# Layer 3's weighted sums of eight heads as 128x64 column tiles in one TensorE run over two PSUM banks

## The chip, the cores and the metric

The kernel runs on one core of a Trainium2 chip. The metric is device time in microseconds (us) of that core for one launch. The median of three runs of the kernel before is 3227.3 us (3219.42 to 3229.8). A core has four engines that compute (TensorE, called PE in the profile; VectorE, DVE; ScalarE, ACT; GpSimd, POOL) and SyncE (SP), which here only issues DMAs. Each runs its own queue of instructions in order. A matrix product on TensorE is two kinds of instruction: a weight load (LDWEIGHTS, shown as PEld) of the operand called `lhsT`, and a MATMUL that streams the other operand, `rhs`, past it into a bank of PSUM. All data here is fp32, for which one matrix product of the program becomes two weight loads and two MATMULs, so the counts in the profile are twice those in the code.

## The reference, cut to what matters

Four graph attention layers run one after another on 128 independent graphs of 128 nodes with 512 features, each as `x = x + layer(relu(layernorm(x)))`. The change is in layer 3, which has eight heads (H = 8) of 64 features (k = 64):

```
xp = jnp.einsum('bnd,do->bno', x, W_proj)
xh = xp.reshape(B, N, H, k).transpose(0, 2, 1, 3)
a_src = jnp.einsum('bhnk,hk->bhn', xh, W_att[:, :k])
a_dst = jnp.einsum('bhnk,hk->bhn', xh, W_att[:, k:])
scores = a_src[:, :, :, None] + a_dst[:, :, None, :] + b_att[None, :, None, None]
scores = jax.nn.leaky_relu(scores, negative_slope=NEG_SLOPE)
mask = (A > 0)[:, None, :, :]
scores = jnp.where(mask, scores, NEG_INF)
att = jax.nn.softmax(scores, axis=-1)
out = jax.nn.relu(jnp.einsum('bhij,bhjk->bhik', att, xh))
return out.transpose(0, 2, 1, 3).reshape(B, N, H * k)
```

The changed step is the last einsum: for each graph and each head, a 128x128 matrix of attention weights times a 128x64 matrix of features.

## The kernel before, in words

A graph is handled whole: its 128 nodes lie on the 128 partitions, and one graph passes through all four layers in a coroutine (`graph`, line 1053), which yields one step at a time. Up to 13 graphs (`FLYING`) are in flight together. The order in which the instructions of all of them are put into the queues is made when the program is built, by a list scheduler (`Scheduler`, line 158): it keeps an estimate of when each engine is free and when each buffer is written, and takes among the steps that could start next on an engine the one of best rank, where a step's rank comes from its graph's number and its due time in a rehearsed plan. The estimates come from `Step.estimate` (line 70); for a PE product it returns `2 * max(0.00084 * columns, 0.108)` us (line 85). A `Group` (line 106) is a list of steps that is issued in one go, with nothing of another graph between them. A buffer is asked for with `Take` and freed with `give_back`; the eight PSUM banks are one such pool (`bank()`, line 387).

`layer3` (line 909) does, for one graph: the normalisation; four transposes of `h`; the projection (`projected`, tiles `bank<-wpx,ht` in the profile) into `fx`, which holds per head two score columns, 64 features and a column of ones; the scores of all heads in one tile `e` of 128x1024; mask, leaky ReLU and exponential on DVE and ACT; and a transposition of `e` by DMA and DVE (by TensorE for the last five graphs, `late`). Then `et[k]` is the transposed 128x128 matrix of head k.

The weighted sums follow (lines 985 to 1009). They go in two halves of four heads. For each half one bank is taken, and one `Group` of four products is issued: `lhsT` is `et[k]` (128x128, as weights), `rhs` is `fx[:, k, E3:]` (65 columns: the features and the ones, whose sum is the softmax's denominator), the result 128 partitions by 65 columns. In the profile these are `bank<-x,e` with 128x65, or `bank<-x,ht` for the last five graphs. When a half is in its bank, DVE takes the reciprocal of the four denominators (line 1002) and multiplies (line 1003) into `t`, and the bank is given back before the coroutine asks for the second. Each graph has two such halves, so the kernel has 256 groups of four products, 1024 products, 2048 weight loads and 2048 MATMULs of this kind. The scheduler may put other graphs' work between the two halves, and mostly does.

Other names that stand below: `bank<-w1x,ht` is layer 1's projection, `bank<-et,xl` its weighted sums, `bank<-w2x,y` its second projection, `bank<-h,et` and `bank<-x,et` the weighted sums of the layers with one head, `bank<-ident,h` transposes. All instructions of the coroutines carry line 310 in the profile (312 in the changed file), since the scheduler issues them there, so they are told apart by their tiles.

Of the kernel before, what the change touches and what calls it, by code (L numbers as in the profile page):

```python
# [42 lines left out]
def size(ap):  # L43
    n = 1
    for count in ap.shape[1:]:
        n *= count
    return n


class Step:  # L50
# [19 lines left out]
    def estimate(self, name, outs, ins, kw):  # L70

        if name == "dma_start":
            moved = size(outs[0]) * outs[0].shape[0] * 4
            if self.engine == "POOL":
                self.moves = moved / 165e3
                return 1.0, 3
            run = 4 * min(a.shape[-1] for a in outs + ins)
            self.moves = moved / (280e3 if run > 512 else 220e3 if run > 128 else 130e3)
            busy = 0.5 if max(len(a.shape) for a in outs + ins) > 2 else 0.35
            return busy, (2.2 if moved > 16384 else 1.3)  # L80
        n = max(size(a) for a in outs[:1] + ins)
        if self.engine == "PE":
            if name == "transpose":
                return 0.109, 0.2
            return 2 * max(0.00084 * size(outs[0]), 0.108), 0.2
        if self.engine == "DVE":
            if name == "bn_stats":
                return 0.6, 0.12
            if name == "bn_aggr":
                return 0.09, 0.12  # L90
            per = 1 / 960
            if name == "tensor_scalar" and n >= 256:
                per /= 2
            return n * per + 0.07, 0.12
        if self.engine == "ACT":
            pointers = sum(isinstance(kw.get(k), bass.AP) for k in ("bias", "scale"))
            busy = n * 0.00081 + 0.105 + (0, 0.075, 0.135)[pointers]
            return busy + 0.1 * ("accum_out" in kw), 0.15
        if self.engine == "POOL":
            if kw.get("op") == ALU.pow or ALU.pow in kw.get("ops", ()):  # L100
                return 0.6, 0.1
            return (0.25 if n <= 16 else 0.55 if name == "tensor_scalar" else 1.3), 0.1
        raise ValueError(name)
# [54 lines left out]
class Scheduler:  # L158
# [14 lines left out]
    def give_back(self, *aps):  # L173
        for ap in aps:
            name = ap.tensor.name
            tag = self.tag_of.pop(name)
            heapq.heappush(self.returned[tag], self.last_use.get(name, 0.0))
# [157 lines left out]
def kernel(  # L335
# [24 lines left out]
    B, P, D = x.shape  # L360
# [4 lines left out]
    H3 = l3_watt.shape[0]  # L365
    K3 = l3_watt.shape[1] // 2
# [12 lines left out]
    T = Engine("PE", nc.tensor)  # L379
# [5 lines left out]
    give_back = sched.give_back  # L385

    def bank():
        return Take(ps, [P, 512], "bank", 8)

    def tile_of(tag, bufs, *shape):  # L390
        return Take(work, [P, *shape], tag, bufs)
# [15 lines left out]
    E1, E2, E3 = 2 * H1, 2, 2  # L407
# [151 lines left out]
    def norm_relu(xt):  # L559

        n = nc.vector.BN_STATS_DIM
        st = yield tile_of("st", 6, n + 5)
        yield V.bn_stats(st[:, :n], xt)
        mean, var = st[:, n : n + 1], st[:, n + 1 : n + 2]
        yield V.bn_aggr(st[:, n : n + 2], st[:, :n])
        ve, rstd, nmr = (st[:, i : i + 1] for i in range(n + 2, n + 5))
        yield G.tensor_scalar(ve, var, EPS, None, ALU.add)
        yield G.tensor_tensor(out=rstd, in0=ve, in1=minus_half, op=ALU.pow)
        yield G.tensor_scalar(nmr, mean, rstd, -1.0, ALU.mult, ALU.mult)
        h = yield tile_of("h", 4, D)  # L570
        yield A.activation(out=h, in_=xt, func=AF.Relu, bias=nmr, scale=rstd)
        give_back(st)
        return h
# [14 lines left out]
    def blocks_of(t):  # L588

        return [t[:, i : i + P] for i in range(0, t.shape[1], P)]  # L590
# [318 lines left out]
    def layer3(xt, mask, late):  # L909

        h = yield from norm_relu(xt)
        ht = yield from transposed(blocks_of(h), "ht", 3)
        give_back(h)
        yield Until("wp")

        fx = yield tile_of("x3", 3, H3, E3 + K3 + 1)
        yield G.memset(fx[:, :, E3 + K3 :], 1.0)
        half = H3 // 2
        yield from projected(
            ht,  # L920
            KC,
            [w.rearrange("p h k -> p (h k)") for w in wpx],
            2,
            [fx[:, g : g + half, : E3 + K3] for g in (0, half)],
        )
        give_back(ht[0])
        f = yield tile_of("f3", 4, 4, H3)
        f, mx, rz = f[:, :2], f[:, 2], f[:, 3]
        yield G.tensor_tensor(f, fx[:, :, :E3].rearrange("p h s -> p s h"), b_l3, ALU.add)

        e = yield tile_of("e3", 3, H3 * P)
        if late:
            heads = e.rearrange("p (h c b) -> p h c b", h=H3, b=Q)
        else:
            heads = e.rearrange("p (c h b) -> p h c b", h=H3, b=Q)
            rows = yield from rows_in_dram(repeated(f[:, 0]), H3)
            yield S.dma_start(out=e.rearrange("p (c f) -> p c f", c=R), in_=rows)
        mask3 = mask.rearrange("p (c b) -> p c b", b=Q)

        for g in range(0, H3, 4):  # L940
            part = [heads[:, g + j] for j in range(4)]
            if late:
                pt = yield from spread(f[:, 0, g : g + 4])
                part = pt.rearrange("p (h c b) -> p h c b", h=4, b=Q)
                part = [part[:, j] for j in range(4)]
            yield Group(
                [
                    V.tensor_tensor_reduce(
                        out=heads[:, g + j],
                        in0=part[j],  # L950
                        in1=mask3,
                        scale=1.0,
                        scalar=LOWEST,
                        op0=ALU.add,
                        op1=ALU.max,
                        accum_out=mx[:, g + j : g + j + 1],
                    )
                    for j in range(4)
                ]
            )  # L960
            if late:
                give_back(pt)
        give_back(mask)
        yield G.tensor_tensor(mx, mx, f[:, 1], ALU.add)
        yield A.activation(out=mx, in_=mx, func=AF.Prelu, alpha=SLOPE)
        yield G.tensor_scalar(mx, mx, -1.0, None, ALU.mult)
        for bias, func in ((f[:, 1], dict(func=AF.Prelu, alpha=SLOPE)), (mx, dict(func=AF.Exp))):
            for k in range(H3):
                yield A.activation(
                    out=heads[:, k], in_=heads[:, k], bias=bias[:, k : k + 1], **func  # L970
                )
        et = []
        if late:
            for g in range(0, H3, 4):
                et += yield from transposed(blocks_of(e)[g : g + 4], "ht", 3)
        else:
            to = yield from exchanged(e, "et3", 2)

            yield V.transpose(
                e.rearrange("p (h r b) -> p r h b", h=H3, b=Q),  # L980
                to.rearrange("p (r h b) -> p r h b", h=H3, b=Q),
            )
            give_back(to)
            et = blocks_of(e)
        t = yield tile_of("t", 5, D)
        for i in range(2):
            pa = yield bank()
            p3 = pa[:, : half * (K3 + 1)].rearrange("p (h k) -> p h k", h=half)
            yield Group(
                [  # L990
                    T.matmul(
                        p3[:, k - i * half, :],
                        lhsT=et[k],
                        rhs=fx[:, k, E3:],
                        start=True,
                        stop=True,
                    )
                    for k in range(i * half, (i + 1) * half)
                ]
            )  # L1000
            r = rz[:, i * half : (i + 1) * half]
            yield V.reciprocal(r, p3[:, :, K3])
            yield V.tensor_tensor(
                t[:, i * half * K3 : (i + 1) * half * K3].rearrange("p (h k) -> p h k", k=K3),
                p3[:, :, :K3],
                r.unsqueeze(2).to_broadcast([P, half, K3]),
                ALU.mult,
            )
            give_back(pa)
        give_back(e, fx, f)  # L1010
        if late:
            give_back(et[0], et[4])
        yield V.scalar_tensor_tensor(xt, t, 0.0, xt, ALU.max, ALU.add)
        give_back(t)
# [133 lines left out]
```

## Time and profile before

| what | value | where from |
|---|---|---|
| median of three runs | 3227.3 us (3219.42 to 3229.8) | the times |
| time of the profiled execution | 3227.98 us | the times |
| its span, first to last instruction | 3226.2 us | the page |
| mean granted TensorE clock | 0.994 | view of the cores |
| weight loads, busy | 2497.0 us (77%), 15386 instructions | the page |
| ACT busy | 2468.5 us (77%), 7224 | the page |
| POOL busy | 855.9 us (27%), 2313 | the page |
| chain that ended last | PE 91%, DVE 3%, DMA 3%, ACT 1%, issue 1% | the page |
| DVE, reciprocal of four denominators (`f<-bank`) | 256 of 173 ns | groups by form |
| DVE, multiplication of a half (`t<-bank,f`) | 256 of 411 ns | groups by form |

How to read it: the page gives for each engine the time in which it executed something. For PE that is not the same as running at its peak: MATMULs are pipelined, one starts before the one before it has ended, so the time that a MATMUL costs is the distance from its start to the next start (called its pitch below), not its duration. The pitch is read from the timeline, which lists runs of equal instructions with their starts.

### The profile page before, as it was taken

To read this page: it belongs to the slowest core of one execution; us is meant where nothing else is said; L and a number is where in the kernel's file an instruction comes from. 1 tells how busy PE (TensorE), PEld (TensorE's weight loads), DVE (VectorE), ACT (ScalarE), POOL (GpSimd) and SP (SyncE) were. 2 spreads that over 40 slices of the span, in tenths; PEclk is the share of its full clock that TensorE was granted. 3 is DMA by queue.
4 is the path that set the end of the run, shared out by engine and by line. 5 is a ranking of instruction groups with operands and counts; after the bars stand their busy time and mean duration, and the time that the engine had idled before them with its cause. 6 is when DMAs were issued, how large, how long until landed. Compare 5 with 4: busy or idle time off the path is not lost.

```text
span 3226.2 us, 60294 instructions
## 1 busy us (share of the span) xinstructions
PE 3189.4 (99%) x15386; PEld 2497.0 (77%) x15386; DVE 2857.0 (89%) x11663; ACT 2468.5 (77%) x7224; POOL 855.9 (27%) x2313
## 2 busy tenths in 40 slices
PE   8999999999999999999999999999999999999998
PEld 6777777777777777777777777777777777777786
DVE  6888888999998989999998999998999989989876
ACT  5677777778777877777877777777777777778867
POOL 1232222222222222222222222222222222222222
PEclk8999999999999999999999999999999999999999
DMA  6245555556556656655555555555555655555432
GB/s 173 52 114 137 144 143 152 153 150 154 150 144 157 153 141 155 155 144 155 155 146 141 157 153 151 153 152 141 151 151 151 154 150 149 143 159 149 110 101 66
DMA packets 770082, 460.39 MB, mean 143 GB/s; under 512 B 344776, under 2 KB 702408, under 8 KB 769736
## 3 DMA queue, kind: packets, MB, share of 16 engines
q1 hardware_dynamic: 765560, 456.53, 54.6%
q8 instruction: 123, 2.02, 0.3%
q14 instruction: 223, 1.83, 0.2%
q10 hardware_dynamic: 4176, 0.02, 0.1%
HBM read 299.00 MB, written 157.33 MB: 141 GB/s over the span
## 4 chain that ended last, share of the span: by engine, by line
PE 91%; DVE 3%; DMA 3%; ACT 1%; issue 1%; POOL 0%; SPq 0%; ACTq 0%; DVEq 0%; POOLq 0%
PE bank L310 91%; DVE e L310 1%; DMA e<-d 1%; DMA d<-r 1%; DMA row<-d 1%; DMA et<-exchanged 0%; DVE st L310 0%; POOL st L310 0%; SPq L310 0%; DVE products L310 0%; DVE xt L310 0%; ACT e L310 0%; DVE t L310 0%; DVE y L310 0%; ACT ht L310 0%
## 5 line engine op out<-in xcount | busy, mean ns | idle before, releaser
L310 PE MATMUL bank<-w2x,y 128*128 128x257 f32 x4096 | 968.6, 381 | 1.7 <-DVE y L310 1.7
L310 PE MATMUL bank<-w1x,ht 128*128 128x344 f32 x3072 | 953.9, 454 | 2.6 <-ACT ht L310 2.6
L310 PEld LDWEIGHTS bank<-w2x,y 128*128 128x128 f32 x4096 | 763.9, 190 | 157.3 <-issue 32.8
L310 PEld LDWEIGHTS bank<-w1x,ht 128*128 128x128 f32 x3072 | 570.3, 191 | 257.2 <-issue 9.3
L310 ACT ACTIVATE e<-e,f 128x128 f32<-128x128 f32 x2176 | 707.2, 390 | 3.1 <-DVE c L310 3.1
L310 POOL TENSOR_SCALAR st<-st 128x1 f32<-128x1 f32 x1024 | 311.1, 308 | 1185.8 <-DVE st L310 993.9
L310 ACT ACTIVATE e<-e,c 128x128 f32<-128x128 f32 x1408 | 533.1, 394 | 116.9 <-DVE c L310 60.2
L310 PE MATMUL bank<-wpx,ht 128*128 128x264 f32 x2048 | 497.1, 386 | 0.3 <-ACT ht L310 0.3
L310 ACT ACTIVATE h<-xt,st 128x512 f32<-128x512 f32 x512 | 411.3, 810 | 83.9 <-POOL st L310 74.4
L310 PEld LDWEIGHTS bank<-wpx,ht 128*128 128x128 f32 x2048 | 387.8, 190 | 97.9 <-issue 22.2
L310 DVE CUSTOM_DVE_ANT_0 e<-e,m 128x128 f32<-128x128 f32 x1484 | 337.8, 286 | 23.5 <-DMA e<-d 23.3
L310 DVE BATCH_NORM_STATS2 st<-xt 128x6 f32<-128x512 f32 x512 | 340.8, 679 | 0.5 <-DMA xt<-in_x_dram 0.5
L310 POOL TENSOR_TENSOR st<-st,minus_half 128x1 f32<-128x1 f32 x512 | 297.0, 599 | 23.6 <-POOL st L310 0.2
L310 PEld LDWEIGHTS bank<-x,e 128*128 128x128 f32 x1968 | 254.8, 191 | 62.2 <-issue 29.8
L310 PEld LDWEIGHTS bank<-et,xl 128*128 128x128 f32 x2048 | 264.7, 192 | 36.5 <-issue 8.8
L310 PE MATMUL bank<-et,xl 128*128 128x128 f32 x2048 | 270.1, 275 | 0.4 <-ACT et L310 0.4
L310 PE MATMUL bank<-h,et 128*128 128x512 f32 x512 | 263.8, 598 | 3.3 <-ACT et L310 1.9
L310 PE MATMUL bank<-x,e 128*128 128x65 f32 x1968 | 246.8, 268 | 8.5 <-DVE e L310 2.1
L310 ACT COPY xl<-bank 128x344 f32<-128x344 f32 x384 | 167.7, 437 | 108.1 <-PE bank L310 103.9
L310 ACT COPY ht<-bank 128x512 f32<-128x512 f32 x274 | 159.6, 582 | 114.9 <-PE bank L310 113.7
L310 ACT ACTIVATE t<-t 128x512 f32<-128x512 f32 x256 | 160.3, 627 | 88.1 <-DVE t L310 87.3
L310 DVE TENSOR_TENSOR y<-bank,b 128x512 f32<-128x512 f32 x256 | 175.1, 684 | 36.0 <-PE bank L310 34.7
(85 smaller groups left out, 4342.4 us busy)
## 6 DMA issues: line engine op xcount, KB each, us to landing
e<-d SPq DMA_DIRECT2D x123, 512.0 KB
exchanged<-e SPq DMA_DIRECT2D x492, 128.0 KB
et<-exchanged SPq DMA_DIRECT2D x123, 512.0 KB
xt<-in_x_dram SPq DMA_DIRECT2D x128, 256.0 KB
out_dram<-xt SPq DMA_DIRECT2D x128, 256.0 KB
e<-d SPq DMA_DIRECT2D x125, 256.0 KB
exchanged<-e SPq DMA_DIRECT2D x480, 64.0 KB
et<-exchanged SPq DMA_DIRECT2D x120, 256.0 KB
```

The costliest lines, as they stand in the source:

```text
L310: method(*args, **kw)
```

## The change

The two groups of four products become one group of sixteen. Both banks are taken before the group. Each head's product is split by its weights: columns 0 to 63 of `et[k]` give output partitions 0 to 63, columns 64 to 127 give output partitions 64 to 127 of the same bank and columns. So a product has 128x64 weights and a 64x65 result, and its place among the array's columns is given by the output's partitions. The 65 columns of `rhs` are streamed for each half. The order is head by head, low half and high half alternating, first the four heads of one bank, then those of the other. The two reciprocals and the two multiplications on DVE are the same as before; they now both come after the whole group. The planner's estimate gets a price of its own for a product with fewer than 128 output partitions, 0.07 us.

```diff
@@ -82,6 +82,8 @@
         if self.engine == "PE":
             if name == "transpose":
                 return 0.109, 0.2
+            if outs[0].shape[0] < 128:
+                return 0.07, 0.2
             return 2 * max(0.00084 * size(outs[0]), 0.108), 0.2
@@ -983,21 +985,22 @@
         t = yield tile_of("t", 5, D)
-        for i in range(2):
-            pa = yield bank()
-            p3 = pa[:, : half * (K3 + 1)].rearrange("p (h k) -> p h k", h=half)
-            yield Group(
-                [
-                    T.matmul(
-                        p3[:, k - i * half, :],
-                        lhsT=et[k],
-                        rhs=fx[:, k, E3:],
-                        start=True,
-                        stop=True,
-                    )
-                    for k in range(i * half, (i + 1) * half)
-                ]
-            )
+        pas = [(yield bank()), (yield bank())]
+        p3s = [pa[:, : half * (K3 + 1)].rearrange("p (h k) -> p h k", h=half) for pa in pas]
+        yield Group(
+            [
+                T.matmul(
+                    p3s[k // half][lo : lo + P // 2, k % half, :],
+                    lhsT=et[k][:, lo : lo + P // 2],
+                    rhs=fx[:, k, E3:],
+                    start=True,
+                    stop=True,
+                )
+                for k in range(H3)
+                for lo in (0, P // 2)
+            ]
+        )
+        for i, p3 in enumerate(p3s):
             r = rz[:, i * half : (i + 1) * half]
             yield V.reciprocal(r, p3[:, :, K3])
             yield V.tensor_tensor(
@@ -1006,7 +1009,7 @@
                 r.unsqueeze(2).to_broadcast([P, half, K3]),
                 ALU.mult,
             )
-            give_back(pa)
+            give_back(pas[i])
```

The built program has 128 runs of sixteen products with a 64x65 result, one for each graph, and no two of them next to each other; before each stand mostly transposes (`bank<-ident,h`, 55 times), layer 1's projection (30) or a one-head weighted sum (28). Since the estimates changed, the scheduler's order differs from the start on. The instructions of DVE, ACT, POOL and SP are the same in kind and number; only their order differs.

## The prediction

> **What bounds the kernel now.** I read the page's busy times first, then the windows of the middle, the waits of PE, the groups by form, and last the timeline of PE around the products that change.
>
> ```profile
> PE 3189.4 (99%) x15386; PEld 2497.0 (77%) x15386; DVE 2857.0 (89%) x11663; ACT 2468.5 (77%) x7224; POOL 855.9 (27%) x2313
> PE   8999999999999999999999999999999999999998
> ...
> PEclk8999999999999999999999999999999999999999
> ```
>
> PE is busy all along at full granted clock. The windows of the middle (us of the window, then busy time of PE, weight loads, DVE, ACT, POOL) and the list of what PE waited for between 400 and 2900 us say whether that is work or waiting:
>
> ```profile
> 800.00:1600.00 800.00, 800.00 (x3868) 627.97 (x3867) 728.98 (x2993) 627.05 (x1835) 218.05 (x590) 1.00 0.59 151
> ```
>
> ```profile
> PE bank L310 <- DVE y L310: 1.7, 1, 1.7
> PE bank L310 <- ACT h L310: 0.3, 1, 0.3
> ```
>
> In 2500 us PE waited 2.0 us. DVE is next with 729 of 800, ACT 627. So time taken from PE's stream in the middle is taken from the whole, us for us, until PE's share falls to DVE's 91%; and time added to it is added. The whole has 128 graphs, and 3226 / 128 = 25.2 us of PE for each.
>
> Now what the products cost. By form (count, busy time, mean ns of one):
>
> ```profile
> L310 PE MATMUL bank<-w2x,y 128*128 128x257 f32 x4096 | 968.6, 381 | 1.7 <-DVE y L310 1.7
> L310 PE MATMUL bank<-w1x,ht 128*128 128x344 f32 x3072 | 953.9, 454 | 2.6 <-ACT ht L310 2.6
> ...
> L310 PE MATMUL bank<-x,e 128*128 128x65 f32 x1968 | 246.8, 268 | 8.5 <-DVE e L310 2.1 <-issue 2.1 <-POOL st L310 1.5
> ```
>
> Between the two long forms a column costs (454 - 381) / (344 - 257) = 0.84 ns. The durations hold a tail beside the columns, so the price of a run is read from starts:
>
> ```profile
> 1502.30 1.90 PE L310 MATMUL bank<-w2x,y 128*128 128x257 f32 x8
> 1504.04 1.00 PE L310 MATMUL bank<-x,e 128*128 128x65 f32 x8
> 1504.88 1.95 PE L310 MATMUL bank<-w2x,y 128*128 128x257 f32 x8
> 1506.66 0.45 PE L310 MATMUL bank<-w1x,ht 128*128 128x344 f32 x1
> ```
>
> The run `x,e` of four heads (8 MATMULs) goes from 1504.04 to 1504.88: 0.84 us. The run of `w2x,y` after it takes 1.78 us to the next start, the one before `x,e` 1.74: a weight load is still owed when `x,e` ends, some 0.04 to 0.05 us. So a half costs 0.89 us, 111 ns a MATMUL. Its 65 columns are worth 65 x 0.84 = 55 ns, half of that. The other half is the weight load, as these rows show, of a run that began after PE had stood still (MATMULs, then weight loads):
>
> ```profile
> 390.02 1.08 PE L310 MATMUL bank<-x,e 128*128 128x65 f32 x8 [1.81 <-DVE e L310]
> 390.94 0.51 PE L310 MATMUL bank<-w1x,ht 128*128 128x344 f32 x1
> ```
>
> ```profile
> 389.99 0.97 PEld L310 LDWEIGHTS bank<-x,e 128*128 128x128 f32 x8 [2.20 <-POOL f L310]
> 390.88 0.30 PEld L310 LDWEIGHTS bank<-w1x,ht 128*128 128x128 f32 x2
> ```
>
> Eight weight loads take 390.88 - 389.99 = 0.89 us: 111 ns for 128 columns of weights. The products to be changed are bound by loading weights, not by streaming. And loading and streaming do run beside each other: layer 1's sums `et,xl` stream 128 columns (107 ns) with the same load (111 ns), and eight take
>
> ```profile
> 1523.67 1.05 PE L310 MATMUL bank<-et,xl 128*128 128x128 f32 x8
> 1524.56 1.02 PE L310 MATMUL bank<-x,et 128*128 128x512 f32 x2
> ```
>
> 0.89 us, not the sum of both.
>
> **The change, part by part.** *Removed:* two halves for each graph, 2 x 0.89 = 1.78 us, 228 us over 128 graphs.
>
> *Added:* one run of 16 products, 32 loads and 32 MATMULs: 16 pairs of one low and one high half. No row shows a 64-column load; by columns it is 111 / 2 = 56 ns. A MATMUL streams the same 65 columns whatever its weights: 55 ns. Bounds of a pair: 55 ns if the two halves of the array work side by side, 16 x 0.055 = 0.88 us a graph; and 2 x 56 = 111 ns if loads follow each other (MATMULs in turn would need 110), 1.78 us, just what is removed. I take 70 ns, a quarter of the way: the nearest row is `et,xl`, where two instructions of like length cost the longer one plus 4%, and the quarter is for that no row has two tiles. That makes 16 x 0.070 = 1.12 us. (The planner's new price of 16 x 0.07 gives the same sum; it is no measurement.)
>
> *Changes of the array's shape:* each run is entered from full-width work and left to it, 256 changes. No row has one. From below: a transposing product after an ordinary one, the nearest change of mode in the trace, costs nothing (`ident,h` follows `x,e` here, and its four instructions take 0.44 us, 110 ns each, which is the load):
>
> ```profile
> 1526.28 1.00 PE L310 MATMUL bank<-x,e 128*128 128x65 f32 x8
> 1527.12 0.61 PE L310 MATMUL bank<-ident,h 128*128 128x128 f32 x4
> 1527.56 1.06 PE L310 MATMUL bank<-et,xl 128*128 128x128 f32 x8
> ```
>
> From above: the array must empty and begin anew. The tail: eight `w2x,y` begin at 1502.30, are busy for 1.90 and so end at 1504.20, 0.16 after the next start. The new beginning: the run from standstill above took 390.94 - 390.02 = 0.92 against 0.84 us, so 0.08 for a first load that nothing covers, 0.04 for one of 64 columns. Together 0.16 + 0.04 on entry and 0.16 + 0.08 on leaving, 0.44 us a graph. Between 0 and 0.44 I take the two tails alone, 0.32: an array that has to change its shape can hardly do so with results in it, while a load may be begun early.
>
> The skill speaks against the change here and for the choice above. The Trainium skill, "TensorEngine Tiling (Array Packing)", section "Key Properties", says that a change of tiling mode drains TensorE, and that different tiles can load and multiply in parallel. No row of this trace shows either. By its first rule alone the two tails (0.32) would be sure, by its second the pair would be nearer to 55 ns, and the sum 0.88 + 0.32 = 1.20 us, 74 us less than before.
>
> *Moved:* the reciprocal and multiplication of the first half wait for the whole group instead of their own four heads, about half a us later; on DVE, in-order, the scheduler puts other graphs' work before them, and nothing on PE waits for them but the release of banks. Taking two banks at once costs nothing as long as PE finds banks free: among its waits none is for DVE's `t` or `f`, which free these banks. If that cover went, each graph would wait for one half's reciprocal and multiplication, 0.173 + 0.411 = 0.58 us, 75 us in all; I take 0. The scheduler's new order on all engines I cost at nothing too, with 2.0 us of waits in 2500 as the cover, and some 5 us either way at the ends, where PE idles 12 us (first 160) and 14 us (last 166). No DMA is added or moved past another but by that order.
>
> *Sum:* 1.12 + 0.32 - 1.78 = -0.34 us a graph, times 128 = -43 us. PE then needs 24.9 us a graph and DVE still 729 / 32 = 22.8 (the window of 800 us holds 32 graphs), so DVE does not take over. Against the profiled execution, 3227.98 - 43 = 3185 us. That execution is 0.7 us above the median of the runs, so no correction.
>
> **The rivals.** A measurement of this kernel can tell about 0.3%, 10 us, from no change.
>
> *A, the forecast:* tiles side by side, with a cost at the changes of shape. 3185; with pairs of 60 to 80 ns and changes of 0.2 to 0.44 it spans 3149 (0.96 + 0.20 - 1.78 = -0.62, -79) to 3220 (1.28 + 0.44 - 1.78 = -0.06, -8). 0.43.
>
> *B, changes of shape are free*, as the transposes are: 1.12 - 1.78 = -0.66, -84: 3144; with pairs at 55 ns -115: 3113. For it: no gap at any change of form in the trace. Against: all these forms use the whole array. 0.13.
>
> *C, loads in turn and free changes*, or side by side and pairs at 85 to 95 ns with changes at 0.32 to 0.44: 1.78 for 1.78, about 3228. 0.09.
>
> *D, slower: the loads of the two tiles go one after the other.* Place: the weight path, which bounds these products already (111 ns for 128 columns however they are cut). Then the run costs 1.78 as before, the gain is nothing and the changes of shape are pure loss: 0.32 x 128 = 41, so 3269; with 0.44, 56 and 3284. It decides as soon as a pair takes more than (1.78 - 0.32) / 16 = 91 ns. For it: in the trace no two weight loads keep less than a full load's distance inside a run. Against: nothing but that `et,xl` shows the array doing two things at once. 0.35.
>
> *The change does not do what it says:* excluded; the built program has 128 unbroken runs of 16 products of 64x65. *DVE becomes the bound:* it would need PE below 22.8 us a graph, out of reach here.
>
> **How the numbers follow.** The likeliest case is A, 3185 us, its own range 3149 to 3220. Range for 8 in 10: from 3135, which leaves out the better part of B, to 3280, which holds D with both prices of the change but its worst. Faster by over 0.3%: A and B, 0.56; within: C, 0.09; slower: D, 0.35.
>
> **What would show it.** Right: `bank<-x,e` with 64 weight columns and 64x65 results, 4096 MATMULs; in the timeline 32 of them in about 1.1 us, and at each end about 0.16 us beyond the usual pitch of the neighbours; PE still without waits in the middle. Wrong: 32 MATMULs in 1.8 us (loads in turn, D); no extra distance at the ends (B); waits of PE for `t` or `f` (banks).

## The result, and the profile after

| | kernel before | changed kernel |
|---|---|---|
| median | 3228.55 us (4 runs, 3219.42 to 3230.36) | 3311.49 us (4 runs, 3305.72 to 3316.3) |
| ratio | | 1.0262, 95% interval 1.0234 to 1.029 |
| profiled execution, its span | 3227.98, 3226.2 us | 3305.72, 3304.0 us |
| mean granted TensorE clock | 0.994 | 0.983 |

The kernel became 2.6% slower, 83 us, and the time lies above the predicted range. The busy times of the page of the changed kernel:

```profile
PE 3173.2 (96%) x17434; PEld 2410.9 (73%) x17434; DVE 2845.3 (86%) x11663; ACT 2455.8 (74%) x7224; POOL 889.6 (27%) x2313
```

PE is busy for 16 us less than before, in a span that is 78 us longer. The products themselves, by form (MATMULs, then weight loads):

```profile
L312 PE MATMUL bank<-x,e 128*64 128x65 f32 x3936 | 141.8, 225 | 4.5 <-DVE e L312 1.9 <-issue 1.7 <-PE bank L312 0.9
```

```profile
L312 PEld LDWEIGHTS bank<-x,e 128*64 128x64 f32 x3936 | 125.0, 137 | 52.6 <-issue 30.5 <-POOL st L312 19.6 <-POOL f L312 1.4
```

(The other 160 of 4096 are `x,ht`, those of the last five graphs. The profile writes a tile's result as 128x65 too; `128*64` are the weights.) One run in the timeline of PE, then of its weight loads:

```profile
1504.75 0.60 PE L312 MATMUL bank<-ident,h 128*128 128x128 f32 x4
1505.28 1.15 PE L312 MATMUL bank<-x,e 128*64 128x65 f32 x32
1506.37 1.12 PE L312 MATMUL bank<-x,et 128*128 128x512 f32 x2
1507.33 0.38 PE L312 MATMUL bank<-w2x,y 128*128 128x257 f32 x1
```

```profile
1505.28 1.01 PEld L312 LDWEIGHTS bank<-x,e 128*64 128x64 f32 x32 [0.17 <-issue]
```

The same view cut off at 1505.33, and then at 1505.38, shows how the loads begin:

```profile
1505.28 0.14 PEld L312 LDWEIGHTS bank<-x,e 128*64 128x64 f32 x2 [0.17 <-issue]
```

```profile
1505.28 0.20 PEld L312 LDWEIGHTS bank<-x,e 128*64 128x64 f32 x4 [0.17 <-issue]
```

They begin in twos, by the trace's single starts 6 or 7 ns apart, and so do the MATMULs. The 32 loads are busy for 1.01 us; less 0.14 for the last two that is 0.87 us for 15 distances, 58 ns a pair. A full-width load took 111. So two half-width tiles are loaded and multiplied side by side. The run goes from 1505.28 to 1506.37, 1.09 us. The four transposes before it take 0.53 us instead of their 0.44, so entering costs 0.09; the two `x,et` after it take 0.96 instead of 0.86 (from 1524.56 to this row in the trace of before), so leaving costs 0.10:

```profile
1525.42 1.02 PE L310 MATMUL bank<-h,et 128*128 128x512 f32 x2
```

With 16 x 0.058 = 0.93 for the pairs, 0.16 of the run's 1.09 belongs to its ends too (by my reading the first load that nothing covers, and the last MATMULs that must be through), 0.35 us for the two changes of shape. Altogether 1.28 us, which is also the mean of the 114 runs that met no wait and no lowered clock. The prediction has 1.78 for the two full-width runs, which would make it 0.50 us a graph. But 0.89 for a half is the dearer case: over the 238 undisturbed halves in the trace of before the mean is 0.86, so 1.73 for two and a saving of 0.45 us a graph, 57 us over 128 graphs. That is more than the forecast's 0.34. The tiles do what they were meant to do.

The time went elsewhere. The waits of PE between 400 and 2900 us, of which the kernel before had 2.0 us:

```profile
PE bank L312 <- DMA et<-dealt: 46.9, 15, 4.1
PE bank L312 <- DVE e L312: 29.8, 10, 4.9
PE bank L312 <- ACT h L312: 6.1, 11, 1.0
PE bank L312 <- DMA et<-exchanged: 0.7, 1, 0.7
PE bank L312 <- ACT ht L312: 0.2, 1, 0.2
```

Together 83.7 us. The long ones come some 102 us apart, once in four graphs. One of them, in the views of SP's issues, of DVE and of PE (in square brackets the idle time before an instruction and what ended it), and then in windows of 5 us (last figures: granted clock, DMA share, GB/s):

```profile
1866.11 0.37 SPq L312 DMA_DIRECT2D e<-d  x1
...
1867.13 0.38 SPq L312 DMA_DIRECT2D row<-d  x1
1867.60 0.38 SPq L312 DMA_DIRECT2D et<-exchanged  x1
1868.03 0.42 SPq L312 DMA_DIRECT2D out_dram<-xt  x1
1868.56 2.85 SPq L312 DMA_DIRECT2D dealt<-e  x1
1871.46 0.49 SPq L312 DMA_DIRECT2D xt<-in_x_dram  x1
1872.95 3.94 SPq L312 DMA_DIRECT2D et<-dealt  x2
```

```profile
1874.32 0.38 DVE L312 CUSTOM_DVE_ANT_1 e<-row,m 128x128 f32<-128x128 f32 x1 [5.28 <-DMA row<-d]
```

```profile
1877.48 1.69 PE L312 MATMUL bank<-h,et 128*128 128x512 f32 x2 [3.69 <-DMA et<-dealt]
1878.97 1.35 PE L312 MATMUL bank<-w1x,ht 128*128 128x344 f32 x2
```

```profile
1870.00:1875.00 5.00, 3.78 (x22) 3.21 (x20) 0.68 (x3) 1.47 (x5) 0.00 (x0) 1.00 0.99 201
1875.00:1880.00 5.00, 2.52 (x4) 1.29 (x5) 4.93 (x16) 2.65 (x9) 0.00 (x0) 0.78 0.38 99
1880.00:1885.00 5.00, 5.00 (x17) 3.14 (x15) 4.26 (x14) 3.17 (x10) 1.27 (x4) 0.87 0.36 72
```

SP issues a small transfer, `row<-d` (64 KB), at 1867.13, behind one of 256 KB (`e<-d`, here 512 rows of 512 bytes) and ahead of one of 512 KB (`et<-exchanged`) and two of 256 KB (`out_dram`, `xt`), and the 16 DMA engines are 99% busy after that. All 20 places where DVE waits over 4 us for a row have this pattern, with the 512 KB issued 0.5 us and the store 0.9 us after the row. DVE stands still for 5.28 us until the row is there, and since its queue is in order, so does all that stands behind. PE runs out of work a little later, in front of the sum of a one-head layer, for 3.69 us. And then it is slow: two `h,et` take from 1877.48 to 1878.97, 1.49 us instead of 0.86, and the granted clock is 0.78 and 0.87 in the next two windows. DVE's waits for `row<-d` alone (between 400 and 2900 us) rose fourfold, from the first of these lines, in the kernel before, to the second:

```profile
DVE e L310 <- DMA row<-d: 30.5, 41, 2.9
```

```profile
DVE e L312 <- DMA row<-d: 132.5, 47, 5.4
```

In sum, over the whole span: tiles -57; PE's idle time, the span less the busy time of the page, 3304.0 - 3173.2 = 130.8 us against 3226.2 - 3189.4 = 36.8, +94, of which 82 are the waits above; clock not granted, (1 - 0.983) x 3304 = 56 us against (1 - 0.994) x 3226 = 19, +37. That makes +74 of the 78 us between the two spans. It is no exact sum, since a little of the time at a lowered clock is idle time too.

### The profile page after: what moved, and what is told of

It is laid out like the page before. It is cut to its first block, busy times and chain, and to the rows that moved or that the text cites. A ratio compares the mean times of both kernels' runs of the same rounds, so it can differ in the third digit from the quotient of the medians.

```text
span 3304.0 us, 64216 instructions
## 1 busy us (share of the span) xinstructions
PE 3173.2 (96%) x17434; PEld 2410.9 (73%) x17434; DVE 2845.3 (86%) x11663; ACT 2455.8 (74%) x7224; POOL 889.6 (27%) x2313
## 4 chain that ended last, share of the span: by engine, by line
PE 36%; DVE 31%; DMA 19%; ACT 8%; issue 4%; SPq 1%; POOL 1%; DVEq 0%; ACTq 0%; POOLq 0%
PE bank L312 36%; DVE e L312 10%; DMA row<-d 6%; ACT e L312 5%; DVE products L312 4%; DVE st L312 3%; DVE xt L312 3%; DVE y L312 3%; DMA e<-d 3%; DMA d<-r 3%; DVE t L312 2%; DMA exchanged<-e 2%; DMA dealt<-e 2%; DVE c L312 2%; DMA et<-dealt 2%
## 5 line engine op out<-in xcount | busy, mean ns | idle before, releaser
L312 PE MATMUL bank<-w1x,ht 128*128 128x344 f32 x3072 | 977.6, 462 | 6.0 <-ACT ht L312 5.9
L312 PEld LDWEIGHTS bank<-w1x,ht 128*128 128x128 f32 x3072 | 582.7, 195 | 277.9 <-issue 29.0
L312 ACT ACTIVATE e<-e,f 128x128 f32<-128x128 f32 x2176 | 716.9, 390 | 28.3 <-DVE c L312 28.2
L312 POOL TENSOR_SCALAR st<-st 128x1 f32<-128x1 f32 x1024 | 318.1, 312 | 1396.1 <-DVE st L312 1225.2
L312 PE MATMUL bank<-h,et 128*128 128x512 f32 x512 | 278.5, 627 | 81.7 <-DMA et<-dealt 50.5
L312 POOL TENSOR_TENSOR st<-st,minus_half 128x1 f32<-128x1 f32 x512 | 321.4, 630 | 37.3
L312 DVE CUSTOM_DVE_ANT_1 e<-row,m 128x128 f32<-128x128 f32 x361 | 136.3, 382 | 182.1 <-DMA row<-d 145.4
L312 PEld LDWEIGHTS bank<-ident,h 128*128 128x128 f32 x1024 | 125.6, 141 | 122.8 <-issue 54.3
L312 DVE SCALAR_TENSOR_TENSOR xt<-bank,c,xt 128x512 f32<-128x512 f32 x256 | 183.1, 724 | 11.9 <-PE bank L312 11.1
```

The lines of the kernel that those rows point to most:

```text
L312: method(*args, **kw)
```

## The experiments

The question was what made PE wait: the new order of all the work, which the planner's estimates determine (theory S), the tiles themselves (T), or the one run that takes two banks (M). The scheduler's order depends on a step's planned length and not on its instructions, so kernels can be made that share an order and differ in the products, and the other way round. For e1 and the changed kernel, for e2 and e3, and for e4 and the kernel before, the built programs have the same order on all five engines.

**e1_full_new_order: the tiling alone undone, order kept.**

```diff
-            if outs[0].shape[0] < 128:
-                return 0.07, 0.2
+            if size(outs[0]) == 65:
+                return 0.14, 0.2
...
-                    p3s[k // half][lo : lo + P // 2, k % half, :],
-                    lhsT=et[k][:, lo : lo + P // 2],
+                    p3s[k // half][:, k % half, :],
+                    lhsT=et[k],
...
-                for lo in (0, P // 2)
```

> Full-width products (128x128 weights, 128x65 results) in one run of eight over two banks, priced 0.14 us each, so that every engine's order is exactly that of the changed kernel; only the tiling of the products is undone. Theory S (the new order makes PE wait, the tiles themselves are faster): the PE waits stay, and the run costs 1.78 instead of 1.28 us, partly in the shadow of those waits: 3311 to 3375 us, well above the kernel before. Rival T (the 64-column tiles or the changes of array shape slow the program, the order is harmless): back near the kernel before, 3218 to 3238 us.

3351.36 us, ratio 1.0391 (1.0373 to 1.0409). Full-width products, in the new order, are 126 us slower than the same products in the old one (3225.55 in these runs), so the tiles aren't what costs the time. Against the changed kernel it is 40 us: that is what the tiles save in this order. PE's waits between 400 and 2900 us are 64.5 us, 19 less than with the tiles, headed by

```profile
PE bank L312 <- DMA et<-dealt: 29.7, 11, 4.2
PE bank L312 <- DVE e L312: 26.2, 11, 3.1
```

By the pages PE is busy for 3238.0 us in e1 and for 3173.2 with the tiles, 65 less, and idle for 105.3 and 130.8, 25 more: a part of what the tiles save comes back as waiting.

**e2_tiled_old_price and e3_full_one_run_old_price: one run at the old price, with and without tiles.** e2 is the changed kernel with one number changed; e3 has in addition the full-width products of e1, at 0.216.

```diff
             if outs[0].shape[0] < 128:
-                return 0.07, 0.2
+                return 0.108, 0.2
```

> The changed kernel with its planner price for a 64-column product at 0.108 us instead of 0.07, so that a group of sixteen is planned at the 1.73 us of the two old groups. Theory S with the price as the cause: the waits go, and the tiles' saving shows: 16 pairs of 58 ns and about 0.35 us at the ends against 1.78, -0.5 us a graph, -64 us: 3150 to 3185 us. Rival M (the single group that holds two banks is what disturbs the order): waits stay, above 3280 us. Rival T (the tiles slow the program): above 3280 us.

> Full-width products at the old price, but all eight in one run over two banks: the merge alone, in exactly the order of the kernel with tiles at the old price. Theory S with the price as the cause, and rival T: as the kernel before, 3218 to 3245 us. Rival M (one run and two banks are the cause): above 3290 us.

e2 3296.97 us, 1.0216 (1.0193 to 1.024); e3 3302.15 us, 1.024 (1.0221 to 1.026). The price of 0.07 alone isn't the cause: the old price with one run gives another order, and it is nearly as slow. e3 looked like rival M: no tiles, the old price, only the merge, and 2.4% lost. Between e3 and e2 the tiles gain nothing that is clear of the noise: PE's waits grow from 40.3 to 87.1 us.

**e4_tiled_halves_before_order: tiles in the order of the kernel before.** Two runs of four heads with one bank each, as before; each head is split in two.

```diff
+            if outs[0].shape[0] < 128:
+                return 0.108, 0.2
...
-                        p3[:, k - i * half, :],
-                        lhsT=et[k],
+                        p3[lo : lo + P // 2, k - i * half, :],
+                        lhsT=et[k][:, lo : lo + P // 2],
...
+                    for lo in (0, P // 2)
```

> Exactly the order of the kernel before on every engine, two runs of four heads, one bank each, but each head as two 64-column tiles. Theory S: no new waits, and each half costs 8 pairs of 58 ns plus some 0.35 us at its ends, about 0.81 against 0.89 us: -20 us, 3195 to 3220 us. Rival T (tiles or changes of shape cost the time): there are twice as many changes as in the changed kernel, so above 3311 us.

3212.29 us, 0.9961 (0.9948 to 0.9974): faster, by 13 us, with 512 changes of the array's shape instead of 256. T has fallen. A half as it stands in the timeline:

```profile
1501.66 0.69 PE L312 MATMUL bank<-x,e 128*64 128x65 f32 x16
1502.28 0.65 PE L312 MATMUL bank<-ident,h 128*128 128x128 f32 x4
```

0.62 us for the run; with what it costs its neighbours the mean of 233 undisturbed halves is 0.79, where the pairs alone are 8 x 0.058 = 0.46. The ends (0.32) are paid for each half, so a half saves only 0.08 of the 0.86 above, 20 us over all by this sum.

**e5_one_run_planned_as_halves: the run on the chip, the plan of before.** The planner sees the two old halves; the first issues all sixteen products, the second none.

```diff
+        run[0].calls, run[1].calls = run[0].calls + run[1].calls, []
         for i, p3 in enumerate(p3s):
+            yield run[i]
             r = rz[:, i * half : (i + 1) * half]
```

> The changed kernel's run on the chip (sixteen 64-column tiles in one go, both banks taken first) under the order of the kernel before: the planner still sees two halves of 0.864 us, the first issues all sixteen products, the second none. The order of all other work equals that of the kernel before but for the last few graphs. Theory S (the planned order is the cause, the run on the chip is sound): no waits, -0.5 us a graph: 3150 to 3180 us. Rival M (a long run that holds two banks is itself what makes PE and DVE wait): above 3280 us.

3211.06 us, 0.994 (0.9921 to 0.9958). Rival M has fallen as well: the same run of sixteen over two banks is faster than the kernel before once the order of the rest is that of before. It is faster than both kernels of the change, and by its ratio the fastest of the study, though its interval overlaps e4's. The gain is less than the forecast of 3150 to 3180. PE's waits, 16.3 us in all:

```profile
PE bank L312 <- DMA et<-exchanged: 9.9, 15, 1.3
PE bank L312 <- ACT h L312: 5.2, 11, 0.9
```

By the pages PE is busy for 48 us less than in the kernel before (3141.5 against 3189.4) and idle for 25 us more (61.5 against 36.8); 14 of the 25 are in these waits, the rest outside 400 to 2900. So about half of what PE saves reaches the time.

**e6_before_price_022, e9_before_price_0212: the order alone.** The kernel before with one line added, no instruction changed; e9 the same with 0.212.

```diff
+            if size(outs[0]) == 65:
+                return 0.22, 0.2
             return 2 * max(0.00084 * size(outs[0]), 0.108), 0.2
```

> The kernel before, nothing changed but the planner's price of its 128x65 products: 0.22 instead of 0.216 us (their measured cost is 2 x 0.111). It changes the order in places and no instruction. Theory O (any order but the one that the constants were set for costs tens of us): above 3245 us. Theory G (it needs the merge into one group of 1.7 us to spoil the order): 3215 to 3240 us.

> The kernel before with the planner's price of its 128x65 products at 0.212 instead of 0.216 us: the other direction of the run at 0.22, no instruction changed. Theory O (any order but the one that the constants were set for costs tens of us): above 3260 us. Rival U (only a higher price, which delays the plan, hurts): 3210 to 3245 us.

e6 3402.09 us, 1.0533 (1.0516 to 1.0551); e9 3264.39 us, 1.0076 (1.0053 to 1.0099). A price that differs by 4 ns for one kind of step makes the kernel 5.3% or 0.8% slower. The first is twice the whole effect of the change, and it doesn't need the merge, so theory G has fallen. Rival U falls too, since e9's interval is clear of 1; but the kernel before ran at 3237.8 in e9's runs, and at the times of e6's runs the ratio would give 3255 us, between the two forecasts. In e6 PE waits 95.5 us, nearly all here:

```profile
PE bank L312 <- DMA et<-exchanged: 92.9, 25, 5.5
```

with a granted clock of 0.974. By the pages PE is idle for 103 us more than in the kernel before (139.4 against 36.8) and busy for 67 us more (3256.5 against 3189.4) with the same instructions, together the 170 us between the spans. The clock that was not granted, 88 us against 19, is worth about that.

**e7_tiled_halves_price_010, e8_tiled_one_run_price_008, e10_tiled_one_run_price_010: more orders.** e7 is e4 with 0.1 for 0.108; e8 and e10 are the changed kernel with 0.08 and 0.10.

> Two runs of four heads as 64-column tiles, as in the run that was 16 us faster, but priced 0.10 us a product, about their measured cost, so that the order moves a little. Theory O: above 3230 us. Theory G: 3195 to 3225 us.

> The changed kernel with a price of 0.08 us a product, 16 x 0.08 = 1.28 us, which is what the run measured in the changed kernel's trace. Theory P (the price of 0.07 is too low, and a true price gives a good order): 3160 to 3200 us. Theories O and G: one more order made with the merged group, 3260 to 3330 us.

> The changed kernel with a price of 0.10 us a product, 1.6 us a run: one more order for the same instructions. Theory O: a draw like the other orders of this run (3297 at 0.108, 3311 at 0.07, 3331 at 0.08), 3270 to 3400 us. Rival P (a price between the true 0.08 and the old 0.108 gives a good order): 3160 to 3220 us.

e7 3368.94 us, 1.0427 (1.0411 to 1.0443); e8 3331.4 us, 1.0324 (1.0302 to 1.0346); e10 3304.85 us, 1.0199 (1.0176 to 1.0223). e4 and e7 have the same instructions and differ by 4.7%. A price that is true to what the run takes (e8) is no better than one that isn't, and one between it and the old one (e10) is no better either: both times rival or theory P has fallen.

| order made with | products | time, us | ratio to the kernel before in the same runs | PE waits 400 to 2900, us | granted clock |
|---|---|---|---|---|---|
| halves at 0.216 (before) | full width | 3227 | 1 | 2.0 | 0.994 |
| the same (e4) | tiles, two runs | 3212 | 0.9961 | 3.3 | 0.994 |
| the same (e5) | tiles, one run | 3211 | 0.994 | 16.3 | 0.992 |
| halves at 0.212 (e9) | full width | 3264 | 1.0076 | 25.1 | 0.993 |
| halves at 0.22 (e6) | full width | 3402 | 1.0533 | 95.5 | 0.974 |
| halves at 8 x 0.10 (e7) | tiles, two runs | 3369 | 1.0427 | 102.9 | 0.977 |
| one run at 1.73 (e3) | full width | 3302 | 1.024 | 40.3 | 0.990 |
| the same (e2) | tiles | 3297 | 1.0216 | 87.1 | 0.988 |
| one run at 1.12 (e1) | full width | 3351 | 1.0391 | 64.5 | 0.983 |
| the same (changed kernel) | tiles | 3311 | 1.0262 | 83.7 | 0.983 |
| one run at 1.28 (e8) | tiles | 3331 | 1.0324 | 99.2 | 0.984 |
| one run at 1.60 (e10) | tiles | 3305 | 1.0199 | 83.4 | 0.987 |

Where two kernels have one order, the tiles are the faster ones in e4, e5 and the changed kernel; between e3 and e2 the intervals overlap. All seven other plans gave an order that is worse than that of before. What the tiles take from PE's stream does not reach the time whole; by the pages (span less busy time is idle time):

| order | PE busy, full width to tiles, us | PE idle, us | span, us |
|---|---|---|---|
| of before, e4 | 3189.4 to 3167.1 | 36.8 to 40.9 | -18 |
| of before, e5 | 3189.4 to 3141.5 | 36.8 to 61.5 | -23 |
| of e3 and e2 | 3220.4 to 3162.3 | 77.8 to 133.4 | -2.5 |
| of e1 and the changed kernel | 3238.0 to 3173.2 | 105.3 to 130.8 | -39 |

**What in a bad order makes PE wait.** The period of four graphs pointed to the adjacency, which is loaded for four graphs at a time; in e6 its four block-transposed loads kept SP busy for 4.8 us shortly before PE's wait. e11 is e6 and e12 the changed kernel, both with these loads replaced:

```diff
+        rows = adj[b : b + AG].rearrange("g i j -> i g j")
+        step.calls = [
+            (nc.sync.dma_start, (), dict(out=t[m * Q : (m + 1) * Q], in_=rows[m * Q : (m + 1) * Q]))
+            for m in range(R)
+        ]
```

> The kernel before at price 0.22 (3402 us), same order on every engine, but the four DMAs for every four graphs that load the block-transposed adjacency (runs of 128 bytes, 4.8 us of issuing on SP just before PE waits there) load plain rows (runs of 512 bytes, the same bytes), so layer 1's mask is another one. Theory A (these loads hold up SP's queue, and the row and exchange transfers behind them come late): below 3340 us. Rival B (the order is bad at other places too): above 3370 us.

> The changed kernel, same order on every engine, with the same plain-row adjacency load, so layer 1's mask is another one. Its PE waits come some 70 us away from these loads, where a 512 KB, a 512 KB and two 256 KB transfers are issued within 5 us. Theory B (each order has its own bad spot): no change, 3290 to 3320 us. Theory A (the adjacency loads are the bad spot of every order): below 3260 us.

e11 3413.06 us, 1.0538 (1.0514 to 1.0561); e12 3328.51 us, 1.0277 (1.0257 to 1.0297). No gain in either, though the four issues took 1.9 us at the place that I looked at. Theory A has fallen: by the ratios, which take out that the kernel before ran slower in these runs too (3237.8), e11 stands where e6 stood (1.0533) and e12 where the changed kernel stood (1.0262), within the intervals. What was left in e11 at that place was a transfer of 0.5 KB, issued behind 1.3 MB, for which SP waited 3.4 us. So the bytes were tried: the result is stored in its first 32 columns only, 16 KB instead of 256 for each graph, in the changed kernel (e13), the kernel before (e14) and e6 (e15).

```diff
+        step.calls = [(nc.sync.dma_start, (), dict(out=out[b][:, :Q], in_=xt[:, :Q]))]
```

> The changed kernel, same order, but each graph's result is stored in its first 32 columns only (16 KB instead of 256 KB). Theory Q (in the bad spots small transfers, on which DVE and then PE wait, land behind some 1.3 to 1.5 MB of large ones issued just before): the burst is a sixth shorter, PE waits and time fall by 20 to 50 us: 3260 to 3292 us. Rival B (the waits follow from the order of DVE, SP and PE alone, not from the bytes): 3300 us or more.

> The kernel before with the same small store, its order unchanged: the control. PE waited 2.0 us in 2500 there, so fewer bytes can gain nothing: 3215 to 3235 us under both theories.

> The kernel before at price 0.22 (3402 us), same order, with the small store. Theory Q: 3340 to 3385 us. Rival B: 3395 us or more.

e13 3270.57 us, 1.0124 (1.0103 to 1.0144): 41 us less than the changed kernel, half of its loss. e14 3227.42 us, 0.9995 (0.9984 to 1.0006): nothing. e15 3391.55 us, 1.0499 (1.048 to 1.0519): 11 us less than e6, between the two theories, and the intervals touch. PE's waits in e13, 69.6 us instead of 83.7, with DVE's share down from 29.8:

```profile
PE bank L312 <- DMA et<-dealt: 46.9, 21, 4.0
PE bank L312 <- ACT h L312: 13.1, 16, 1.2
PE bank L312 <- DVE e L312: 8.0, 6, 2.4
```

and the clock is 0.989 for 0.983. So in the changed kernel's order the bytes of the stores are a part of the cause, and shown as such by e13 against e14; in e6's order they are a small part at most. But they don't act quite as the expectations have it, of which e12's counts two transfers of 512 KB here and e13's puts the large ones before the small one: the store is issued behind the row at all 20 places. The row is used 7.0 us after its issue there in the mean of the changed kernel and 6.3 in e13, and DVE's waits for `row<-d` fell only from 132.5 to 119.2 us; where DVE waited for a row in the kernel before, it was 3.3 us in the median. PE's waits for `et<-dealt` are 46.9 us with the whole store and with the small one. What the 512 KB beside the store do was not tried. The rest of what makes an order bad stays open; that the order of the changed kernel is what cost the time is shown by e1 and e5.

## Why the prediction was wrong

- *What bounds the kernel* was read rightly as far as PE and its weight loads go: e4 became faster by the tiles alone. That time taken from PE's stream is taken from the whole, "us for us", did not hold: e4 got 18 us of 22, e5 23 of 48, the changed kernel against e1 39 of 65, and e2 against e3 2.5 of 58, all in the profiled executions of the table above. PE's share of the span was 96% to 99% in them, DVE's 85% to 89%.
- *The pair of tiles*, 70 ns between 55 and 111: 58 measured, near the lower bound. The rule of the Trainium skill, "TensorEngine Tiling (Array Packing)", "Key Properties", that different tiles load and multiply in parallel, agrees with the 58 ns. Rival D (loads in turn, 111) has fallen.
- *The changes of shape*, 0.32 us a graph between 0 and 0.44: 0.35. The same section's rule of a drain at a change of mode agrees with that: it is about what the prediction's rows give for an emptied array. Rival B (free) has fallen.
- *The sum for PE's stream*, -0.34 us a graph, was -0.45: the pairs were 0.19 cheaper than taken (0.93 for 1.12), the ends 0.03 dearer, and the two halves removed were worth 1.73 instead of 1.78.
- *Two banks at once*, costed at nothing: right for the changed kernel and e5, where none of PE's waits between 400 and 2900 us is for `t` or `f`. In other orders it isn't quite nothing: 2.9 us of such waits in e3, 6.8 in e10.
- *The step that failed* is one sentence: "The scheduler's new order on all engines I cost at nothing too, with 2.0 us of waits in 2500 as the cover". The cover was a property of that very order, not of the kernel: e6 has the same instructions, another order, and 95.5 us of waits. I took the absence of waits in one order as slack that any order would have. That DVE at 91% of the same window, and the four dependent transfers of each one-head layer (`d<-r`, `row<-d`, `dealt<-e`, `et<-dealt`), left little is my reading, which no run tests by itself. The step was given some 5 us either way where the runs show, by their ratios, +0.8% to +5.3% for full-width products (e9, e3, e1, e6).
- *The range* ended at 3280 because only D and its ends stood above. Slower had 0.35, but by a mechanism that the 58 ns refute; the one that decided wasn't among the rivals, though the built program told that the order differed from the start on.
- *What would show it*: the signs named for A (32 MATMULs in about 1.1 us) came true, those of D and of the banks did not, and "PE still without waits in the middle" was the one that failed.

## What to carry to other kernels

Where a list scheduler with hand-set constants makes the order, an edit of a price or a step's length is two changes: what it does to its own instructions, and a new draw of the order of everything else. Price the second by its own row of runs (here a change of 4 ns in one price cost 0.8% and 5.3%), or keep the old order by planning the new step at the old lengths, as e5 does, before judging the first. An engine that is 99% busy without waits says what the present order is worth; it isn't slack that a new order inherits, and a saving on that engine is an upper figure for the whole (here between a twentieth and four fifths of it arrived).

## What the runs showed of the hardware that was not expected

A wait of PE can cost more than its length. After the 3.69 us above the clock was granted at 0.78 and 0.87 over the next two windows of 5 us, and two 512-column MATMULs took 1.49 us instead of 0.86. In the slow orders but e9's (0.993) the mean clock is 0.990 to 0.974 for 0.994, and in e6 PE is busy for 67 us more beside 103 us more of idle time. The Trainium skill, "TensorE: Matmul & The Clock Gate", Part 1, states that PE falls back to half its clock after an idle window of some 3.4 us. The wait of 3.69 us agrees with that. e3 doesn't: no wait of PE between 400 and 2900 us is longer there than 2.1 us, and yet the clock fell, as here:

```profile
1350.18 1.13 PE L312 MATMUL bank<-et,xl 128*128 128x128 f32 x8 [2.07 <-DVE t L312]
1351.15 3.44 PE L312 MATMUL bank<-w2x,y 128*128 128x257 f32 x8
1354.39 1.79 PE L312 MATMUL bank<-w1x,ht 128*128 128x344 f32 x5
```

```profile
1352.00:1354.00 2.00, 2.00 (x7) 1.54 (x6) 2.00 (x9) 1.37 (x5) 0.00 (x0) 0.50 0.74 195
```

After a wait of 2.07 us the clock is granted at 0.50, and eight `w2x,y` take 3.24 us instead of 1.74. So in these runs a shorter idle time was enough at some places. It wasn't everywhere: after the one wait of 1.7 us in the middle of the kernel before the clock stayed at 1.00.

Two 64-column fp32 tiles with the same 128 rows take 58 ns for a pair of loads and a pair of MATMULs, where one full-width load took 111; entering this shape and leaving it cost 0.35 us together. With four heads in a run (e4) such ends are 0.32 of its 0.79 us, with eight 0.35 of 1.28.
